# A two-layer graph network on one core: the stretch ahead of the first gather rebuilt, and layer 0's drain reordered

## The chip, the cores and the metric

The kernel runs on one core of a Trainium2 chip. The time is the device time of one execution in microseconds, as the median of several executions; a profile is one execution recorded by the hardware profiler. The core's engines run their own instruction streams and meet at semaphores: PE (matrix product), DVE (vector), ACT (scalar functions), POOL (which here mostly issues gathers) and SP (which issues most DMAs).

## The reference, cut to what matters

The graph has 6250 nodes with 128 features and 106250 edges, sorted by destination. Both layers are computed as `x = x + layer(relu(layernorm(x)))`.

```python
# layer 0: attention over the incoming edges (GATv2)
xl = h @ Wl + bl;  xr = h @ Wr + br
m  = leaky_relu(xl[src] + xr[dst] + edge_weight1 @ We, 0.2)
logits = m @ att
ex    = exp(logits - segment_max(logits, dst)[dst])
alpha = ex / (segment_sum(ex, dst)[dst] + 1e-16)
out = gelu(h + segment_sum(xl[src] * alpha[:, None], dst) + bias_out)   # then a batch norm over all nodes
# layer 1: messages
em = relu(layer_norm(concat(h[src], h[dst]) @ msg_w + msg_b)) * edge_weight
messages = segment_mean(em, dst)
h_new = relu(layer_norm(concat(h, messages) @ upd_w + upd_b));  out = gate * h_new + (1 - gate) * h
```

## The kernel before

**First stretch (L212 to L454).** The nodes are taken in 17 batches of up to three tiles of 128 rows. For batch i a loop over i = 0..18 issues `normal(i)` (ACT makes the normalized rows, L327, and PE transposes them, L328), `product(i - 1)` (ACT copies the transposes, L332, and PE multiplies, L335) and `table(i - 2)` (ACT or DVE copies the product to `tl`, L342, and SP writes it to the DRAM table `xl_d`, L345). Between them stand steps of four generators. `work` (`squeezing`) removes the self loops from the rows of source indices `ed_r`, 99 blocks of 1078 edges: it makes the masks `moves` (L282) and shifts by predicated copies in seven levels (`squeeze`, L210). `stats` makes the layer norm's statistics on DVE (L308, L310). `seen` (`checks`) lets POOL and ACT test whether the graph has the form that the fast code needs, into twelve numbers `bad`; `said` (`verdict`) sums them to a `flag`. `columns_of(q)` transposes the squeezed rows on PE (L415), and DVE turns them into index columns `src_c` (L417, L418). All of it is issued in program order, so the order of the code is the order on each engine.

**Two arms.** Then all engines read the flag, and `tc.If(usual != 0)` (L1798, L1799) runs `fast()`, the Else arm `general()`. The general arm holds some 16,500 instructions and does not run here.

**Set-up of the fast arm (L1030 to L1110).** DVE computes each block's first node (`first_i`, L1045) and relative destinations (`dl_b`, written to `dl_d`), squeezes the edge weights `ea_r` (L210), and makes the tables of `xr` in three bfloat16 parts (`xr_rows`, L1000 to L1006, to `xr_d`); ACT casts the weights to three parts (L1074 to L1083), which SP writes eightfold to `ea_d` (1.58 MB, three DMAs). `load(table, s)` brings a block's node rows (`W`), its destinations (`oht`, 240 KB) and its weight rows (`load_weights`, L1022); `one_hot_t` (L1026) turns the destinations into a transposed one-hot on DVE. SP issues these loads in order with everything else that it sends.

**Layer 0's loop (L1377 to L1457).** 99 blocks s, one round each, and LAG + 1 = 8 rounds more to drain. In a round POOL issues eight gathers of 128 rows of `xl_d` (`gl`, L185); PE expands `xr[dst] + e` (L1124); DVE adds the gathered rows (L1412), ACT applies Relu (L1413), DVE multiplies with `att` (L1422), sums (L1424) and adds (L1425, L1428) to the logits `lgc`. `one_hot_t(s + 2)` stands on DVE between L1412 and L1422 of block s. Four blocks make a batch; `maxima(b)` finds the segment maxima and exponentials of a batch in steps over several rounds (PE `mx` L1165, DVE `lt` L1168, scans, `cc` L1195, `exm` L1208). Seven rounds behind the gathers, block u = s - LAG is aggregated: DVE makes its one-hot `oh` (L1393) and, with ACT, the weighted rows `glw` (L1400 to L1407), PE sums (L1437), ACT copies (L1297) and SP stores to one of two tables `res` (L1127). Groups of four node tiles are finished as their sums are complete (`nodes(g)`, L1216 to L1279): SP fetches `fin`, DVE computes, PE transposes, ACT applies Gelu.

Gathers are paced: with `PACED = 3`, the even gathers of block s wait for successive marks of block s - 3.

```python
marks = passed.get(s - PACED, ())
if j % 2 == 0 and j // 2 < len(marks):          # marks: L1412, L1422, L1428, L1393 of block s - 3
    tc.add_manual_dep(row.ins, marks[j // 2].ins.name, ...)
```

`breaks()` and `late_columns()` are generators whose steps are taken one per round from round 0 on: they prepare the segment boundaries (`fst_d`, `brk_d`, `kbrk`, `brks`), small vectors (`cols`) and the columns of the self loops' weights. Each step sends DMAs on SP's queue, and the first five rounds also send four DMAs of zeros (`res`, 327 KB each).

**The drain.** In the eight last rounds nothing is gathered; the last maxima, the last seven aggregates and the last three node groups (four, three and two tiles) are left. After the loop `in_turn` interleaves the last two groups. A short middle part (batch norm, tables for layer 1) follows, and then layer 1's loop, which is built like layer 0's, with its own gathers from `a_d`.

Of the kernel before, what the change touches and what calls it, by code (L numbers as in the profile page):

```python
# [66 lines left out]
def kernel(  # L67
# [45 lines left out]
    moves = state.tile([NS, 7, BE], U8, name="moves")  # L113
# [3 lines left out]
    own_r = state.tile([NS, RE], F32, name="own_r")  # L117
# [94 lines left out]
    with tc.tile_pool(name="pre", bufs=3) as pp, tc.tile_pool(name="pre1", bufs=1) as p1, tc.tile_pool(  # L212
# [135 lines left out]
        def checks():  # L348
# [5 lines left out]
            acc = p1.tile([NS, 3], F32, name="acc")  # L354
# [3 lines left out]

            place = p1.tile([NS, BE], F32, name="place")
            behind = p1.tile([NS, BE], F32, name="behind")  # L360
            GP.iota(place, pattern=[[1, BE]], base=0, channel_multiplier=0, allow_small_or_imprecise_dtypes=True)
            GP.tensor_scalar(behind, dst_r[:, :BE], base_f, None, op0=ALU.subtract)
            GP.tensor_tensor(place, place, behind, ALU.subtract)
            GP.tensor_scalar(place, place, float(CH), None, op0=ALU.is_le)
            GP.tensor_tensor(place, place, step[:, :BE], ALU.mult)
# [26 lines left out]
            S.activation(junk[:, :BE], place, AF.Copy, accum_out=acc[:, 2:3])  # L392
            GP.tensor_tensor(q, far[:, 0:1], acc[:, 2:3], ALU.subtract)
            GP.tensor_scalar(bad[:, 11:12], q, float(NW - 1), None, op0=ALU.is_gt)
# [6 lines left out]

        def verdict():
            flag_ps = ps_k.tile([1, 12], F32, name="flag_ps", tag="ctp")
            T.matmul(flag_ps, ones[:NS, 0:1], bad, start=True, stop=True)
            yield
            V.tensor_reduce(sum_, flag_ps, AX.X, ALU.add)
            V.tensor_scalar(sum_, sum_, 0.0, None, op0=ALU.is_equal)
            yield
            S.copy(flag, sum_)
# [23 lines left out]
        for i in range(n + 2):  # L433
            if i % 2 and (i + 1) // 2 in rstds:
                scales((i + 1) // 2)
            if i < n:
                normal(i)
            next(stats, None)
            next(work, None)
            if i % 3 == 2:  # L440
                next(work, None)
            if 1 <= i <= n:
                product(i - 1)
            if i == 14:
                for _ in work:
                    pass
            if i in (15, 16):
                columns_of(i - 15)
            if i in (1, 4, 9):
                next(seen)  # L450
            if i >= 11:
                next(said, None)
            if i >= 2:
                table(i - 2)  # L454
# [469 lines left out]
    def fast():  # L924
# [10 lines left out]
        ea_d = dram.tile([NS * 8 * SE], BF16, name="ea_d")  # L935
        base_d = dram.tile([NS * 2], I32, name="base_d")
# [45 lines left out]
        gate = fs.tile([P, NT], F32, name="gate")  # L982
        bns = fs.tile([P, NGR, 6], F32, name="bns")
# [36 lines left out]
        def load_weights(s):  # L1020

            nc.sync.dma_start(ohts[s % 3][KW:P, :], flat(ea_d, [[SE, 8], [1, SE]], s * 8 * SE))  # L1022
# [6 lines left out]
        wins = {}  # L1029
        with tc.tile_pool(name="col1", bufs=1) as p1, tc.tile_pool(name="ps_p", bufs=2, space=PSUM) as ps_p, tc.tile_pool(  # L1030
            name="ps_x", bufs=1, space=PSUM
        ) as ps_x, tc.manual_schedule():
# [19 lines left out]
            squeeze(ea_r, 0)  # L1052
            made = xr_rows(p1, ps, 0)
            next(made)
            for k in range(1, 3):
                squeeze(ea_r, k)
                V.tensor_tensor(we_l, We_r if k == 1 else we_l, we_p[:, k - 1, :], ALU.subtract)
                S.copy(we_p[:, k, :], we_l)
                next(made, None)
# [9 lines left out]
            for k in range(3, 7):  # L1069
                squeeze(ea_r, k)  # L1070
# [13 lines left out]
            for k, (r0, n) in enumerate(((0, 3), (3, 3), (6, 2))):  # L1084
                nc.sync.dma_start(flat(ea_d, [[8 * SE, NS], [SE, n], [1, SE]], r0 * SE),
                                  ea_p[k][:, None, :].to_broadcast([NS, n, SE]))
            for s in range(2):
                load_weights(s)
                one_hot_t(wins[s][1])
            columns(ps_p, eac_c, ea_r, "ctp")  # L1090
# [60 lines left out]
        with tc.tile_pool(name="e0", bufs=2) as ep, tc.tile_pool(  # L1151
# [3 lines left out]
        ) as ps_m, tc.tile_pool(name="ps_1", bufs=1, space=PSUM) as ps_1, tc.manual_schedule():  # L1155
            (iota_ps,) = constants(ps_1)
            LAG = SB + 3
            gls, lgc, exm, pss, aggs, passed = {}, {}, {}, {}, {}, {}

# [56 lines left out]
            def nodes(g):  # L1216
# [44 lines left out]
                for j in range(n):  # L1261
# [38 lines left out]
            def breaks():  # L1300
# [8 lines left out]
                V.tensor_scalar(cut, fst, -BIG, None, op0=ALU.mult)  # L1309
                nc.sync.dma_start(flat(fst_d, [[SE, NS], [1, SE]]), cut)  # L1310
                yield
# [7 lines left out]
                nc.sync.dma_start(flat(brk_d, [[ST, NS], [NS * ST, 3], [1, ST]]), brk)  # L1319
                V.memset(kbrk[:, :, 0:1], 0.0)  # L1320
                V.memset(kbrk[:, :, P : P + 1], 0.0)
                for b, m, n in ((0, NBT, NS // SB), (NS // SB, NS % SB * ST, 1)):
                    if m:
                        nc.sync.dma_start(kbrk[:m, b : b + n, 1:P],
                                          flat(fst_d, [[P, m], [P * NBT, n], [1, P - 1]], b * P * NBT + 1))
                for q in range(2):
# [3 lines left out]
                    S.copy(fst_c[:, :, q * 4 : (q + 1) * 4].rearrange("p s j -> p j s"), tp)  # L1330
                yield
# [8 lines left out]
            def late_columns():  # L1340

                def column(o, a):
# [9 lines left out]
                    yield  # L1352
                V.tensor_add(bias_c, bias_c, bl_c)
                V.tensor_add(wlr, w0[:, :D], w0[:, D:])
                yield from column(own_c[0], own_r)
# [8 lines left out]
                V.tensor_add(wab, w1[:, :D], w1[:, D : 2 * D])  # L1364
                yield
# [11 lines left out]
            for s in range(NS + LAG + 1):  # L1377
# [11 lines left out]
                if 0 <= u < NS:  # L1389
                    b, q = divmod(u, SB)  # L1390
                    m = tiles(u)
                    oh = ep.tile([P, ST, P], F32, name="oh")
                    made_oh = V.tensor_tensor(oh[:, :m, :], over_tiles(iota_ps, m),  # L1393
                                              over_features(dl_c[:, u, :m], m), ALU.is_equal)
                    if s <= NS:
                        passed[s - 1].append(made_oh)
                    if q == 0:
                        next(steps, None)
# [15 lines left out]
                if u < 0 or u % SB:  # L1414
                    next(steps, None)
# [15 lines left out]
                if s + 2 in early:  # L1431
                    made = xr_rows(np_, xp, early[s + 2])
                    next(made)
                if 0 <= u < NS:
# [3 lines left out]
                if s % SB == SB - 1 and s // SB < BT:  # L1438
                    steps = maxima(s // SB)
                next(steps, None)  # L1440
# [10 lines left out]
                if s < 3:  # L1451
                    next(begun)
                else:
# [9 lines left out]
        cen = fs.tile([P, P], F32, name="cen")  # L1463
        V.tensor_scalar(cen, ident, -1.0 / D, None, op0=ALU.add)
        avg = fs.tile([P, 1], F32, name="avg")
        V.memset(avg, 1.0 / D)
        wm = fs.tile([P, D + 1], F32, name="wm")
        V.tensor_copy(wm[:, :D], w1[:, :D])
        V.tensor_copy(wm[:, D:], w1[:, 3 * D : NW1])
# [13 lines left out]
        fx.enter_context(tc.manual_schedule())  # L1483
# [314 lines left out]
    usual = nc.values_load(flag[0:1, 0:1], min_val=0, max_val=1)  # L1798
    with tc.If(usual != 0) as arm:  # L1799
        fast()  # L1800
    with arm.Else():
        general()
# [41 lines left out]
```

## Time and profile before

| what | us |
|---|---|
| median of 3 runs (2247.89 to 2249.55) | 2247.99 |
| the profiled execution | 2248.83 |
| its span | 2247.0 |
| DVE / POOL / ACT / PE busy | 1697.3 / 1575.9 / 1283.9 / 1160.8 |
| first gather of layer 0 | 69.31 |
| last gather of layer 0 ends | 1084.83 |
| last logits (L1428 of block 98) | 1091.41 |
| batch norm's aggregate (L1491) | 1145.69 |
| first gather of layer 1 | 1193.53 |
| last output issued | 2240.88 |

The span runs from the first to the last instruction of the record; the execution's own time lies 1.83 us above it. Times on a timeline are from the span's start. A timeline row gives start, duration, engine, line and operation, `out<-in` by tile names, and in brackets how long the engine stood idle before the row and what released it. A row with x2 or more is several equal instructions in sequence. A row of waits reads: who waited for whom, total us, number of waits, the longest.

### The profile page before, as it was taken

The numbers are of one execution on the slowest core, as the hardware profiler recorded it, in microseconds if no ns is written. First come the engines' busy times: TensorE is split into PE (matmuls) and PEld (weight loads), VectorE is DVE, ScalarE is ACT, GpSimd is POOL, SyncE is SP. The second block draws the span as 40 slices with busy tenths as digits, with TensorE's granted clock in tenths as the row PEclk, the third lists the DMA queues.
The fourth block names the chain that finished last, engine by engine and source line by source line (L and its number), as shares of the span: only waits on it lengthen the run. The fifth ranks groups of instructions, "written<-read, shape, count | busy, mean of one in ns | idle before, by whom it ended". The sixth has DMA issues, their size and how long they took to land. (4 is left out here: it accounts for less than half of the span.)

```text
span 2247.0 us, 28217 instructions
## 1 busy us (share of the span) xinstructions
PE 1160.8 (52%) x6261; PEld 1032.2 (46%) x6261; DVE 1697.3 (76%) x3898; ACT 1283.9 (57%) x4314; POOL 1575.9 (70%) x1637
## 2 busy tenths in 40 slices
PE   5215545645555654655673445454554554554454
PEld 4114545544444544544553445454544554544443
DVE  8558887887787787777864677787787787788785
ACT  6214434444443444433435677777787787787774
POOL 6667777777777777777226777777777777777770
PEclk9556666665666566555676666666666665766776
DMA  5463356434444434434223333443443343343341
GB/s 139 143 187 100 94 150 187 123 93 113 114 94 115 111 88 114 118 84 107 49 61 104 87 104 94 106 113 93 107 109 101 96 115 106 87 117 104 95 106 30
DMA packets 243495, 239.16 MB, mean 106 GB/s; under 512 B 90708, under 2 KB 186909, under 8 KB 243315
## 3 DMA queue, kind: packets, MB, share of 16 engines
q1 hardware_dynamic: 192531, 133.21, 21.0%
q0 software_dynamic: 50496, 103.92, 19.7%
q14 instruction: 128, 1.05, 0.2%
q8 instruction: 52, 0.85, 0.2%
q10 hardware_dynamic: 288, 0.13, 0.0%
HBM read 189.20 MB, written 47.90 MB: 106 GB/s over the span
## 5 line engine op out<-in xcount | busy, mean ns | idle before, releaser
L185 POOL DMA_INDIRECT gl<-xl_d,src_c x789 | 767.2, 972 | 267.3 <-issue 162.2
L185 POOL DMA_INDIRECT gl<-a_d,src_c x789 | 752.7, 954 | 248.7 <-issue 166.4
L1437 PE MATMUL agg_ps<-glw,oh 128*128 128x131 f32 x1578 | 342.8, 403 | 217.0 <-ACT agg L1297 154.1
L1437 PEld LDWEIGHTS agg_ps<-glw,oh 128*128 128x128 f32 x1578 | 318.7, 306 | 238.3 <-ACT agg L1297 219.4
L1774 PE MATMUL agg_ps<-glw,oh 128*128 128x130 f32 x1056 | 240.9, 417 | 331.5 <-ACT glw L1765 331.5
L1774 PEld LDWEIGHTS agg_ps<-glw,oh 128*128 128x128 f32 x1056 | 222.5, 314 | 345.5 <-ACT glw L1765 345.5
L1745 ACT ACTIVATE sq<-y 128x128 f32<-128x128 f32 x789 | 243.8, 309 | 107.9 <-DVE y L1737 86.1
L1407 ACT ACTIVATE glw<-gl,exm 128x128 f32<-128x128 f32 x763 | 233.1, 389 | 0.0
L1413 ACT ACTIVATE m_ps<-m_ps 128x1024 f32<-128x1024 f32 (+1 forms) x99 | 99.5, 1005 | 218.0 <-DVE m_ps L1412 109.9
L1412 DVE TENSOR_TENSOR m_ps<-m_ps,gl 128x1024 f32<-128x1024 f32 (+1 forms) x99 | 121.7, 1230 | 123.6 <-DMA gl<-xl_d,src_c 107.3
L1756 DVE SCALAR_TENSOR_TENSOR y<-y,rs,cst 128x128 f32<-128x128 f32 x789 | 211.7, 341 | 0.0
L1774 PE MATMUL agg_ps<-ea_r,oh 128*128 128x130 f32 x522 | 120.4, 421 | 171.3 <-ACT ea_r L1765 171.3
L1124 PEld LDWEIGHTS <-oht 128*128 128x128 bf16 (+1 forms) x1578 | 146.2, 126 | 124.7 <-issue 55.5
L1774 PEld LDWEIGHTS agg_ps<-ea_r,oh 128*128 128x128 f32 x522 | 111.0, 318 | 177.9 <-ACT ea_r L1765 177.9
L1026 DVE TENSOR_SCALAR oht<-oht,third 120x1024 bf16<-120x1024 bf16 x198 | 100.1, 506 | 103.7 <-DMA oht<-dl_d 103.5
L1765 ACT ACTIVATE glw<-y,ew_c 128x128 f32<-128x128 f32 x528 | 161.5, 388 | 0.0
L1422 DVE TENSOR_TENSOR m_ps<-m_ps,att 128x1024 f32<-128x1024 f32 (+1 forms) x99 | 120.9, 1221 | 36.9 <-ACT m_ps L1413 36.2
L1745 ACT ACTIVATION_READ_ACCUMULATOR sq<-y 128x1 f32 x789 | 146.9, 186 | 0.0
L1737 DVE TENSOR_TENSOR y<-y_ps,gl 128x1024 f32<-128x1024 f32 (+1 forms) x99 | 119.4, 1206 | 33.2 <-DMA gl<-a_d,src_c 17.3
L1124 PE MATMUL m_ps<-W,oht 128*128 128x128 bf16 x789 | 89.2, 282 | 101.4 <-DVE lr L1424 83.0
L1761 ACT ACTIVATE y<-y 128x1024 f32<-128x1024 f32 (+1 forms) x99 | 104.3, 1054 | 37.6 <-DVE y L1758 37.6
L1424 DVE TENSOR_REDUCE lr<-m_ps 128x8 f32<-128x1024 f32 (+1 forms) x99 | 120.9, 1221 | 3.4
(329 smaller groups left out, 2247.2 us busy)
## 6 DMA issues: line engine op xcount, KB each, us to landing
oht<-dl_d SPq DMA_DIRECT2D x198, 240.0 KB
gl<-xl_d,src_c POOLq DMA_INDIRECT x789
gl<-a_d,src_c POOLq DMA_INDIRECT x789
res<-zt SPq DMA_DIRECT2D x20, 327.5 KB
res<-zt SPq DMA_DIRECT2D x20, 325.0 KB
res<-agg SPq DMA_DIRECT2D x99, 64.5 KB
res<-agg SPq DMA_DIRECT2D x99, 64.0 KB
W<-xr_d SPq DMA_DIRECT2D x198, 30.0 KB
```

What stands on the lines that cost most here:

```text
L185: return GP.indirect_dma_start(out=dest, out_offset=None, in_=table, in_offset=bass.IndirectOffsetOnAxis(ap=idx, axis=0))
L1124: T.matmul(ps[:, j, :], oht[:rows_, j * P : (j + 1) * P], w[:rows_, j // TN, :], start=True, stop=True)
L1407: S.activation(glw[:, j, :D], glu[:, j, :D], AF.Copy, scale=f)
L1412: passed[s] = [V.tensor_tensor(ps, ps, gl[:, :n, :D], ALU.add)]
L1422: passed[s].append(V.tensor_tensor(ps, ps, over_tiles(att8, n), ALU.mult))
L1424: V.tensor_reduce(lr, ps, AX.X, ALU.add)
L1437: T.matmul(aggs[u], oh[:, j, :], glw[:, j, :], start=(j == 0), stop=(j == m - 1))
L1737: added = V.tensor_tensor(y[:, :n, :], pss.pop(s)[:, :n, :], gl[:, :n, :], ALU.add)
L1745: S.activation(sq, y[:, j, :], AF.Square, accum_out=rs[:, j : j + 1])
L1756: marks.append(V.scalar_tensor_tensor(yu[:, j, :], yu[:, j, :], ru[:, j : j + 1], mg_ps, op0=ALU.mult, op1=ALU.mult))
L1765: S.activation(glw[:, j, :D], yu[:, j, :], AF.Copy, scale=ew_c[:, u, j : j + 1])
L1774: T.matmul(aggs[u], oh[:, j, :], glw[:, j, :], start=(j == 0), stop=(j == m - 1))
```

## The change

It has six parts.

1. `checks` loses the tests that used `place` and `behind` (seven POOL instructions and ACT's sum L392); three small DVE instructions on one column of the squeezed rows take their place in `bad[11]`. The flag now counts violations, `general()` is the If arm and `fast()` the Else arm.
2. In the first stretch the squeezing ends at i = 12 (14 before), `columns_of` stands at 13 and 14 (15 and 16), and the first three of the seven squeezes of `ea_r` move from the fast arm's set-up to i = 16, 17 and 18, ahead of `table(i - 2)`.
3. The weights of the first four blocks go to a table `ea_h` of their own, sent ahead of the whole of `ea_d`, and `load_weights` reads it for s < 4. The whole `ea_d` follows the first two loads.
4. The order written by hand holds from the fast arm's start. `cen`, `avg` and `wm` are made in the last steps of `late_columns`.
5. `breaks` has four steps instead of three, with its DMAs a step later; `late_columns` begins in round 3 beside the fourth.
6. Drain: the last maxima start in round NS, two steps at a time and ahead of the aggregate in PE's order. The one-hots of the last three blocks are made in rounds 85, 87 and 89 into buffers that are free by then. For the last three node groups, two of the three products per node tile go to ACT.

```diff
-            place = p1.tile([NS, BE], F32, name="place")
-            behind = p1.tile([NS, BE], F32, name="behind")
-            GP.iota(place, pattern=[[1, BE]], ...)
-            GP.tensor_scalar(behind, dst_r[:, :BE], base_f, None, op0=ALU.subtract)
-            GP.tensor_tensor(place, place, behind, ALU.subtract)
-            GP.tensor_scalar(place, place, float(CH), None, op0=ALU.is_le)
-            GP.tensor_tensor(place, place, step[:, :BE], ALU.mult)
...
-            S.activation(junk[:, :BE], place, AF.Copy, accum_out=acc[:, 2:3])
-            GP.tensor_tensor(q, far[:, 0:1], acc[:, 2:3], ALU.subtract)
-            GP.tensor_scalar(bad[:, 11:12], q, float(NW - 1), None, op0=ALU.is_gt)
...
+            V.tensor_scalar(half_i, ed_r[:, CH : CH + 1], P - 1, None, op0=ALU.bitwise_and)
+            V.tensor_tensor(more, far[:, 0:1], half_i, ALU.subtract)
+            V.tensor_scalar(bad[:, 11:12], more, float(NW - 1), None, op0=ALU.is_gt)
...
-            if i == 14:
+            if i == 12:
                 for _ in work:
                     pass
-            if i in (15, 16):
-                columns_of(i - 15)
-            if i in (1, 4, 9):
+            if i in (1, 4, 9, 12):
                 next(seen)
-            if i >= 11:
+            if i in (13, 14):
+                columns_of(i - 13)
+            if i >= 16:
+                squeeze(ea_r, i - 16)
+            if i >= 13:
                 next(said, None)
             if i >= 2:
                 table(i - 2)
...
-            nc.sync.dma_start(ohts[s % 3][KW:P, :], flat(ea_d, [[SE, 8], [1, SE]], s * 8 * SE))
+            nc.sync.dma_start(ohts[s % 3][KW:P, :],
+                              flat(ea_h if s < SB else ea_d, [[SE, 8], [1, SE]], s * 8 * SE))
...
-            squeeze(ea_r, 0)
+            squeeze(ea_r, 3)
             made = xr_rows(p1, ps, 0)
             next(made)
             for k in range(1, 3):
-                squeeze(ea_r, k)
...
-            for k in range(3, 7):
+            for k in range(4, 7):
                 squeeze(ea_r, k)
...
+            send(ea_h, 0, SB)
             for s in range(2):
                 load_weights(s)
                 one_hot_t(wins[s][1])
+            send(ea_d, 0, NS)
...
+                if g >= NGR - 3:
+                    for j in range(n):
+                        for o, k in ((fin[:, 1, j, :D], 1), (xl[:, j, :D], 2)):
+                            S.activation(o, o, AF.Copy, scale=mm[:, k, j : j + 1])
+                    for j in range(n):
+                        V.scalar_tensor_tensor(fin[:, 0, j, :D], fin[:, 0, j, :D], mm[:, 0, j : j + 1],
+                                               fin[:, 1, j, :D], op0=ALU.mult, op1=ALU.add)
+                    V.tensor_tensor(fin[:, 0, :n, :D], fin[:, 0, :n, :D], xl[:, :n, :D], ALU.add)
-                for j in range(n):
+                for j in range(n if g < NGR - 3 else 0):
                     V.tensor_scalar(fin[:, 0, j, :D], fin[:, 0, j, :D], mm[:, 0, j : j + 1], None, op0=ALU.mult)
...
                 V.tensor_scalar(cut, fst, -BIG, None, op0=ALU.mult)
+                yield
                 nc.sync.dma_start(flat(fst_d, [[SE, NS], [1, SE]]), cut)
-                yield
...
+                    if q == 0 and s >= NS:
+                        next(steps, None)
+                        if s == NS:
+                            steps = maxima(BT - 1)
+                            next(steps)
+                    elif s > NS:
+                        next(steps, None)
+                        next(steps, None)
+                    oh = ohs.pop(u, None)
+                    if oh is None:
+                        oh = ep.tile([P, ST, P], F32, name="oh")
+                        made_oh = one_hot(oh, u)
...
+                if 85 <= s < 91 and s % 2:
+                    k = (s - 85) // 2
+                    ohs[NS - 3 + k] = rooms[k]
+                    one_hot(rooms[k], NS - 3 + k)
+                if s >= NS:
+                    next(steps, None)
+                    next(steps, None)
                 if 0 <= u < NS:
                     aggs[u] = ps_1.tile([P, WF], F32, name="agg_ps")
...
-    usual = nc.values_load(flag[0:1, 0:1], min_val=0, max_val=1)
-    with tc.If(usual != 0) as arm:
+    special = nc.values_load(flag[0:1, 0:1], min_val=0, max_val=12 * P)
+    with tc.If(special != 0) as arm:
+        general()
+    with arm.Else():
         fast()
-    with arm.Else():
-        general()
```

## The prediction

> **What bounds the kernel now.** I read the page first, then POOL's waits and timeline, then what stands ahead of the first gather, then the drain. Times below are the profiled execution's: span 2247.0, execution 2248.83, which is 0.84 above the median 2247.99.
>
> The page's costliest groups (busy us, mean ns | idle before):
>
> ```profile
> L185 POOL DMA_INDIRECT gl<-xl_d,src_c x789 | 767.2, 972 | 267.3 <-issue 162.2
> L185 POOL DMA_INDIRECT gl<-a_d,src_c x789 | 752.7, 954 | 248.7 <-issue 166.4
> ```
>
> A gather costs 0.94 to 0.95 us and 0.30 of issue, 1.25 in all; 789 of them make 986 us of the 1015.5 us in which layer 0 gathers (69.31 to 1084.83). So layer 0 is POOL's: a microsecond counts if it moves the first gather, opens or closes a gap between gathers, or lies behind the last. DVE, at 76%, mostly does not count. POOL's waits in layer 0 and the rows behind the two long ones:
>
> ```profile
> POOL gl L185 <- DVE first_i L1045: 19.0, 1, 19.0
> POOL gl L185 <- DVE m_ps L1422: 12.1, 13, 8.5
> ...
> 69.31 1.45 POOL L185 DMA_INDIRECT gl<-xl_d,src_c  x1 [18.95 <-DVE first_i L1045]
> ...
> 147.06 0.94 POOL L185 DMA_INDIRECT gl<-xl_d,src_c  x1 [8.46 <-DVE m_ps L1422]
> ```
>
> Bracketed is the idle time before a row and its releaser. The first wait is put down to first_i, but a gather reads xl_d and src_c; DVE's row of the same moment names the landing. From DVE's timeline:
>
> ```profile
> 59.08 0.86 DVE L417 CAST ed_c<-ctp 128x396 int32<-128x396 f32 x1 [6.51 <-PE ctp L415]
> ...
> 64.93 0.29 DVE L342 COPY tl<-mm 128x129 f32<-128x129 f32 x1 [0.48 <-PE mm L335]
> 65.80 0.69 DVE L1039 TENSOR_SCALAR ed_r<-ed_r 99x1024 int32<-99x1024 int32 x1 [0.58 <-issue]
> ...
> 68.41 0.23 DVE L1464 TENSOR_SCALAR cen<-ident 128x128 f32<-128x128 f32 x1 [1.90 <-DMA xl_d<-tl]
> ...
> 145.16 0.48 DVE L1026 TENSOR_SCALAR oht<-oht,third 120x1024 bf16<-120x1024 bf16 x1 [14.07 <-DMA oht<-dl_d]
> 145.57 1.23 DVE L1422 TENSOR_TENSOR m_ps<-m_ps,att 128x1024 f32<-128x1024 f32 x1
> ```
>
> Last table copy 64.93, table landed 68.41, first gather 69.31: 4.4 us from copy to gather. And gather 50 (block 6, third tile; each block's even gathers are paced by block s-3) waits for block 3's L1422, which stands behind a one-hot whose load came late. The drain, again from DVE's timeline:
>
> ```profile
> 1100.67 0.28 DVE L1168 COPY lt<-mx 21x128 f32<-21x128 f32 x1 [4.52 <-PE mx L1165]
> ...
> 1129.25 0.17 DVE L1237 TENSOR_TENSOR own_l<-fin 128x3 f32<-128x3 f32 x1 [4.04 <-DMA fin<-res]
> ```
>
> DVE idles 4.52 because mx is queued on PE behind a node group's eight `up` pairs and an aggregate, and 4.04 because the next group is fetched only when block 96 is stored.
>
> **1. The first stretch.** Seven POOL steps over 99x1078 go, five of them from 18.46 to 32.60 without a break, and ACT's L392 (1.10+0.19). While they run, DVE is slow: L282 takes 1.73, 1.45 and 1.95 (later 0.69 to 0.72), L210 2.83 (next 1.34), L318 0.91 (0.17). Up to 29.3, where ACT waits for DVE for the last time (3.73), that is 1.0+0.75+1.5+0.74 = 4.0 us. From there ACT works without a gap until 58.5, so its end moves by 4.0+1.3 = 5.3, to about 53.2. The columns (L417, L418) come two batches earlier, 1.95 us each, so at about 59.08-5.3-3.9 = 49.9 instead of at the end, where they held table copies back (PE waited 1.80 and 1.92 for them). Their place on DVE is taken by three squeezes of 1.35, 1.37 and 1.42, each ahead of a table copy. DVE from 53.4: copy 0.55, squeeze, copy, squeeze, copy, squeeze, last copy at about 59.3. Plus 4.4: first gather 63.7, **-5.6**. Bounds: -3 if POOL's 2.23 us product (L396), now at about 33, slows DVE there in its turn; -8 if the squeezes fit into DVE's waits. POOL's moved checks end at 50.4 already, so POOL itself waits for nothing new; the three tiny DVE steps are 0.5 us inside the 6.51 that DVE waits.
>
> **2. The branch.** The general arm is now the near one; all engines jump over it. The nearest row is the test without a jump: 0.58 us idle ahead of L1039. For POOL a jump lies inside its wait of 18.95 for the table; for DVE and SP it delays the setup by 0 to 3 us, which section 3 covers. At the end a jump falls away: the last output is issued at 2240.88+0.29, a landing takes about 3.1 (65.27 to 68.41), and the span ends at 2247.0, so at most some 2.7 us can be in it. I take the value nearest the row, **-0.5** (0 to -2.7).
>
> The Trainium skill, "Runtime: NRT & Kernel Launch", section "Instruction fetch mechanics", speaks against this edit: a taken branch out of the two fetched pages stalls until the target page is fetched. By that rule every engine pays at the start what it saved at the end; POOL's share stays hidden, so the total would be the same or lower by that stall. No row here shows a fetch by itself.
>
> **3. The early rounds.** After the branch three squeezes (4.14) are gone from the setup and it starts 5.6 earlier, so the node table xr_d leaves at about 67 (76.32 before). The weights go through a small table of four blocks: its three sends follow the casts (87.15 before, about 77 now), and the first loads need not wait until 1.58 MB have landed (issued 83.2 to 87.5, read at 93.77). First L1412 at about 83 (97.16). The price is queue order: the full 1.58 MB now stand on SP ahead of load(2), so one_hot(2), and L1422(0) behind it on DVE, wait until about 89 (99.46 before). From there the rounds were set by loads: DVE waited 5.62, 7.41 and 14.07 for them, because SP had been held by fst_d (waiting for DVE's cut), brk_d, xr_d, zeros and five small columns. With fst_d and brk_d each sent a round later, load(3) goes past them; I get L1422(1) at 98 (113.1), L1422(2) at 104 (126.5) and, with xr_d, four zeros, brk_d and kbrk now ahead of load(5), L1422(3) at 120 (145.57). Gather 50 is due at 137.66+0.94+0.30-5.6 = 133.3. That leaves 13 us, so the gap of 8.46-0.30 = **-8.1** closes. Bounds: 0 to -8.1. What is late next: gather 58 needs L1422(4), about 131 against 143. The slow first ten gathers (about 7 us above 1.25 each) I leave as they are.
>
> Added to later rounds: three one-hots of 1.22 us in rounds 85, 87 and 89. A round is 10 us of POOL with DVE busy 77%, so 2.3 us are free: 0. The copies for cen, avg and wm, some 0.6 us, likewise.
>
> **4. The drain.** All relative to the same start (L1428 of block 98 at 1091.41). lt no longer waits for the aggregate of 3.48: 1097.4 instead of 1100.67. But one one-hot and its products (2.1 us) that filled DVE before lt now stand behind it, the middle of the maxima waits for the aggregate that is now behind mx (cc about 1101.8, about 1.5 us of idle in two places), and two blocks' one-hot and products lie ahead of the four-tile group's end instead of one. Its products: twelve DVE steps (3.95 from 1113.07) become eight ACT copies of 0.30 with a sum at the end, 2.45+0.7 = 3.15. PE's four transposes, which ran between products, now all wait for the sum: 1.6. I get the aggregate of block 96 at 1118.7 to 1119.4 (1120.02), its end 1121 to 1122.5 (1123.9), and own_l of the three-tile group, 5.4 us behind it by store and fetch, at 1127.3: -1.9. That group then saves 0.4 (2.92 becomes 1.85+0.6). In the two-tile group ACT's products stand behind a table load of 1.28 and a gelu of 0.52 (1140.52 to 1142.33) and PE's transposes behind the sum: +0.7. Drain **-1.6**; bounds +2 (PE slow, ACT in the way) and -7.8 (4.5 of idle and three one-hots, 1.22+1.22+0.82, gone whole).
>
> **Sum.** -5.6-0.5-8.1-1.6 = -15.8; 2248.83-15.8 = 2233.0, and 0.84 less on the scale of the median: **2232**. All behind the drain only moves.
>
> **Rivals.** (a) The gap returns: load(2) behind 1.58 MB, or a jump of 3 us on SP, and L1422(3) arrives after 141.5. Against it are 13 us of slack; for it, that every wait of these rounds was a load. Then -5.6-0.5-1.6 = -7.7: 2240. (b) The drain pays what its edits remove, -7.8 instead of -1.6: 2226. For it, all of DVE's 4.52 is PE's order; against it, the fetch behind block 96. (c) Slower: gathers stretch while DVE copies; beside L210 at 148.7 to 151.5 two took 1.29 and 1.12 instead of 0.94. If the new DVE order (late columns' squeezes, one-hots) stretches layer 0's mean from 972 to above 972+15.8/789 = 992 ns, the gain is gone; at 1000 ns it is 22 us, so 2254. Against it: the long steps are as many as before. (d) The change doesn't do what it says: the table copies stay bound by PE and the first gather stays at 69, with the gap closed: 2238.
>
> **How the numbers follow.** The forecast 0.70, (a) 0.12, (b) 0.08, (c) 0.05, (d) 0.05. The forecast's own bounds in sections 1, 2 and 4 give 2225 to 2239; (b) with the earliest first gather reaches 2223, (a) with its own spread 2243. Differences under 0.2%, 4.5 us, are no change here: faster 0.90, same 0.05, slower 0.05.
>
> **What would show it.** First gather near 63.7; no wait above 1 us on L185 but the first; L1422(3) near 120; gathers ending near 1071; from the last L1428 to bn_aggr 52 to 53 us (54.3 before); L185's mean at 972 or under. I am wrong if the first gather is after 66, if a gap above 3 us stands anywhere in layer 0, or if the drain is longer than before.

## The result and the profile after

| what | before | after | difference |
|---|---|---|---|
| median (4 runs each) | 2247.94 | 2226.64 | ratio 0.9902, 95% interval 0.9885 to 0.9919 |
| lowest and highest | 2246.44, 2249.55 | 2223.24, 2226.99 | |
| the profiled execution; its span | 2248.83; 2247.0 | 2226.99; 2225.2 | span -21.8 |
| first gather | 69.31 | 64.26 | -5.05 |
| layer 0's gathers, first start to last end | 1015.52 | 1006.67 | -8.85 |
| last gather's end to the last logits | 6.58 | 6.66 | +0.08 |
| drain, last logits to the batch norm's aggregate | 54.28 | 52.56 | -1.72 |
| middle, from there to layer 1's first gather | 47.84 | 45.47 | -2.37 |
| layer 1, to the last output's issue | 1047.35 | 1045.39 | -1.96 |
| tail, to the span's end | 6.12 | 4.19 | -1.93 |

The seven stages add up to the span's 21.8. The experiments below ran on three chips. On the second and the third every kernel took about a quarter longer, before included (2795 and 2840), so whole times are compared only within a chip. The extra time lies in the two loops: layer 0's gathers take 1236 to 1260 us there and 1003 to 1010 in the changed kernel and its variants on chips of normal speed, layer 1 takes 1349 to 1385 against 1045 to 1048. The first stretch, the drain and the middle take about what they take elsewhere and are compared across chips.

Of the profile after, first the page's costliest groups, then POOL's waits (who waited for whom, total us, times, longest):

```profile
L187 POOL DMA_INDIRECT gl<-xl_d,src_c x789 | 766.5, 971 | 267.5 <-issue 169.5
L187 POOL DMA_INDIRECT gl<-a_d,src_c x789 | 753.9, 956 | 248.0 <-issue 178.9
```

```profile
POOL gl L187 <- DVE first_i L1050: 27.3, 1, 27.3
```

A gather costs what it cost (971 ns against 972, 956 against 954), and the wait that stood second, 12.1 us for the product with att, has gone. The first wait is longer (18.95 before) only because POOL, without its tests, is idle from 36.93 on instead of 50.36. Two stretches of DVE's timeline, the end of the first stretch and the early rounds:

```profile
51.31 0.88 DVE L414 CAST ed_c<-ctp 128x396 int32<-128x396 f32 x1 [3.70 <-PE ctp L412]
...
58.63 1.42 DVE L212 COPY_PREDICATED ea_r<-moves,ea_r 99x1074 f32<-99x1074 uint8 x1
59.89 0.33 DVE L344 COPY tl<-mm 128x129 f32<-128x129 f32 x1
62.90 0.69 DVE L1044 TENSOR_SCALAR ed_r<-ed_r 99x1024 int32<-99x1024 int32 x1 [2.69 <-issue]
...
94.26 0.57 DVE L1030 TENSOR_SCALAR oht<-oht,third 120x1024 bf16<-120x1024 bf16 x1 [8.77 <-DMA oht<-dl_d]
94.75 1.21 DVE L1461 TENSOR_TENSOR m_ps<-m_ps,att 128x1024 f32<-128x1024 f32 x1
...
128.09 0.49 DVE L1030 TENSOR_SCALAR oht<-oht,third 120x1024 bf16<-120x1024 bf16 x1 [12.15 <-DMA oht<-dl_d]
128.50 1.22 DVE L1461 TENSOR_TENSOR m_ps<-m_ps,att 128x1024 f32<-128x1024 f32 x1
```

The last table copy came 5.04 us earlier (59.89 against 64.93), and the gather followed 4.37 behind it (4.38 before). New is the 2.69 us in which DVE waits for nothing that the profile shows, just where it now jumps over the general arm. The one-hots of the early rounds still wait for their loads, but no gather does. POOL's timeline at the first gathers and at gather 50:

```profile
64.26 1.21 POOL L187 DMA_INDIRECT gl<-xl_d,src_c  x1 [27.33 <-DVE first_i L1050]
...
130.94 0.94 POOL L187 DMA_INDIRECT gl<-xl_d,src_c  x1 [0.30 <-issue]
...
142.70 1.87 POOL L187 DMA_INDIRECT gl<-xl_d,src_c  x1 [0.30 <-issue]
```

Gather 50, which had waited 8.46, starts 0.30 behind its neighbour. Its condition, the product at 128.50, was fulfilled at about 129.7, 1.2 us ahead of it: the gap closed by a hair. The drain, on DVE:

```profile
1083.60 0.28 DVE L1184 COPY lt<-mx 21x128 f32<-21x128 f32 x1 [3.67 <-PE mx L1181]
...
1113.49 0.16 DVE L1253 TENSOR_TENSOR own_l<-fin 128x3 f32<-128x3 f32 x1 [5.05 <-DMA fin<-res]
...
1130.15 0.51 DVE L1530 BATCH_NORM_AGGREGATE bmv<-bns 128x2 f32<-128x78 f32 x1
```

The first idle time shrank from 4.52 to 3.67, the second, for the fetch behind the last but two blocks, grew from 4.04 to 5.05: part of what was taken away came back there.

### The profile page after: what moved, and what is told of

The parts are those of the page before. It is cut to its first block, busy times and chain, and to the rows that moved or that the text cites. A ratio compares the mean times of both kernels' runs of the same rounds, so it can differ in the third digit from the quotient of the medians.

```text
span 2225.2 us, 28204 instructions
## 1 busy us (share of the span) xinstructions
PE 1142.5 (51%) x6261; PEld 1018.4 (46%) x6261; DVE 1688.0 (76%) x3885; ACT 1288.1 (58%) x4330; POOL 1564.2 (70%) x1630
## 5 line engine op out<-in xcount | busy, mean ns | idle before, releaser
L1483 PE MATMUL agg_ps<-glw,oh 128*128 128x131 f32 x1536 | 328.7, 398 | 216.6 <-ACT agg L1321 177.6
L1483 PEld LDWEIGHTS agg_ps<-glw,oh 128*128 128x128 f32 x1536 | 306.4, 302 | 236.8 <-ACT agg L1321 219.4
L1813 PEld LDWEIGHTS agg_ps<-glw,oh 128*128 128x128 f32 x1056 | 221.6, 313 | 349.3 <-ACT glw L1804 349.3
L1452 ACT ACTIVATE m_ps<-m_ps 128x1024 f32<-128x1024 f32 (+1 forms) x99 | 99.5, 1005 | 214.9 <-DVE cc L1211 111.0
L1461 DVE TENSOR_TENSOR m_ps<-m_ps,att 128x1024 f32<-128x1024 f32 (+1 forms) x99 | 120.9, 1221 | 38.8 <-ACT m_ps L1452 38.0
```

What stands on the lines that cost most here:

```text
L1461: passed[s].append(V.tensor_tensor(ps, ps, over_tiles(att8, n), ALU.mult))
L1483: T.matmul(aggs[u], oh[:, j, :], glw[:, j, :], start=(j == 0), stop=(j == m - 1))
L1813: T.matmul(aggs[u], oh[:, j, :], glw[:, j, :], start=(j == 0), stop=(j == m - 1))
```

## The experiments

Each is the changed kernel with one edit or one group of edits, and all compute everything. Times of stages are each from one profiled execution.

**The fast arm near again.**

```diff
+            V.tensor_scalar(sum_, sum_, 0.0, None, op0=ALU.is_equal)
-    special = nc.values_load(flag[0:1, 0:1], min_val=0, max_val=12 * P)
-    with tc.If(special != 0) as arm:
-        general()
-    with arm.Else():
-        fast()
+    usual = nc.values_load(flag[0:1, 0:1], min_val=0, max_val=1)
+    with tc.If(usual != 0) as arm:
+        fast()
+    with arm.Else():
+        general()
```

> The changed kernel with the fast arm as the near one again, as before the change; nothing else. Changed kernel: DVE idle 2.69 us ahead of its first instruction in the arm, first gather 64.26, last output issued 2221.01, span end 2225.2 (4.2 us later; 6.1 in the kernel before). Theory (the jump costs at the start but is hidden for POOL, and its absence saves about 1.9 us at the end): idle ahead of DVE's first step back to about 0.6, first gather within 0.3 of 64.26, last output to end about 6.1, execution 1 to 2 us longer. Rival (the 1.9 us at the end are something else): last output to end stays near 4.2, execution within 1 us.

2230.22 (one run; before on that chip 2250.34). DVE no longer idles behind the last table copy:

```profile
60.45 0.28 DVE L344 COPY tl<-mm 128x129 f32<-128x129 f32 x1
60.64 0.68 DVE L1045 TENSOR_SCALAR ed_r<-ed_r 99x1024 int32<-99x1024 int32 x1
```

and from the last output's issue to the end it takes 6.86 instead of 4.19. So the idle time at 60.2 and the 2.7 us at the end are both the price of a jump, and the one that the change pays is covered: the first gather is at 64.15 against 64.26, the first block's addition (L1452) at 82.84 against 84.26.

**POOL's tests back.** The seven steps with `place` and `behind` and ACT's sum are restored, the three small DVE steps removed; all else as changed.

```diff
+            GP.iota(place, pattern=[[1, BE]], ...)
+            GP.tensor_scalar(behind, dst_r[:, :BE], base_f, None, op0=ALU.subtract)
...
+            S.activation(junk[:, :BE], place, AF.Copy, accum_out=acc[:, 2:3])
```

> The changed kernel with POOL's and ACT's old test (place, behind, L392's sum) back; all else as changed. Theory (DVE runs slow beside POOL's 99x1078 steps, ACT is released late): DVE's masks in the first 33 us take 1.5 to 1.9 us instead of 0.69, first gather 4 to 5 us later than 64.26; the stretch of gathers moves as a whole, gap ahead of gather 50 under 2 us. Rival (the gain of the first stretch is the moved index columns alone): first gather at most 1 us later.

2228.83. The last table copy is at 63.86 and the first gather at 68.36, 4.1 us later than in the changed kernel; no gap appears (gather 50 at 136.15). DVE's first three masks take 1.73, 1.45 and 1.95 again, as before the change (0.69 to 0.73 without the tests). Of the 5.05 at the first gather these tests are therefore some 4; ACT's sum is among them and was not tried alone. About 1 is left for the moved columns and squeezes together.

This run also settles a rival for the closed gap, that only the earlier start of the set-up closes it. Here the set-up starts at 66.84, later than before the change (65.80). The products with att of blocks 0 and 3, in the kernel before and then in this run:

```profile
99.46 1.23 DVE L1422 TENSOR_TENSOR m_ps<-m_ps,att 128x1024 f32<-128x1024 f32 x1 [0.69 <-ACT m_ps L1413]
145.57 1.23 DVE L1422 TENSOR_TENSOR m_ps<-m_ps,att 128x1024 f32<-128x1024 f32 x1
```

```profile
98.73 1.21 DVE L1467 TENSOR_TENSOR m_ps<-m_ps,att 128x1024 f32<-128x1024 f32 x1
132.99 1.23 DVE L1467 TENSOR_TENSOR m_ps<-m_ps,att 128x1024 f32<-128x1024 f32 x1
```

The first comes at nearly the same time, the fourth 12.6 us earlier. What closed the gap lies between the first block and the fourth.

**The three squeezes back in the set-up.**

```diff
-            if i >= 16:
-                squeeze(ea_r, i - 16)
...
-            squeeze(ea_r, 3)
+            squeeze(ea_r, 0)
             made = xr_rows(p1, ps, 0)
             next(made)
             for k in range(1, 3):
+                squeeze(ea_r, k)
```

> The changed kernel with the first three squeezes of the edge weights back in the fast arm's set-up (4.2 us of DVE work ahead of the last table copies gone). Theory (these squeezes, not PE or ACT, set the last table copy): last copy at about 56 instead of 59.89, first gather 3 to 4 us earlier (about 60.7); the set-up is longer by what it starts earlier, so block 3's second step stays near 128.5 and gather 50, due at about 127, waits 2 to 3 us: execution within 2 us of the changed kernel. Rival (PE sets the last copy): first gather within 0.5 of 64.26, block 3's step near 132, gap about 3 us, execution 3 us longer.

2232.68, and neither expectation held. The last table copy came 2.6 us earlier (57.3), yet the first gather did not (64.48). What changed was the next gather, beside two of the returned squeezes. POOL's and then DVE's timeline of this run:

```profile
64.48 2.01 POOL L187 DMA_INDIRECT gl<-xl_d,src_c  x1 [27.51 <-DVE dl_b L1052]
66.80 4.19 POOL L187 DMA_INDIRECT gl<-xl_d,src_c  x1 [0.30 <-issue]
```

```profile
62.32 0.69 DVE L1042 TENSOR_SCALAR ed_r<-ed_r 99x1024 int32<-99x1024 int32 x1 [4.73 <-issue]
...
65.94 1.38 DVE L212 COPY_PREDICATED ea_r<-moves,ea_r 99x1076 f32<-99x1076 uint8 x1
...
68.01 1.38 DVE L212 COPY_PREDICATED ea_r<-moves,ea_r 99x1074 f32<-99x1074 uint8 x1
```

A gather of 0.94 took 4.19, as one did before the change:

```profile
72.32 4.15 POOL L185 DMA_INDIRECT gl<-xl_d,src_c  x1 [0.30 <-issue]
```

From first to eleventh gather it is 20.13 us here, 19.53 before, 15.65 in the changed kernel. The moved squeezes pay by not standing beside the first gathers: 4.5 us. The Trainium skill, "SBUF — State Buffer", section "SBUF: two separate sides", says that POOL cannot write the descriptors of its DMAs while DVE runs an operation in a mode that takes both ports. Its example is an fp32 copy. No run here shows the ports; these rows show a gather stretched beside predicated copies. Not every such copy does it: in the changed kernel two gathers beside the three predicated copies from 71.05 to 73.72 took 0.96 and 0.94.

**One weight table.** The small table's three sends are gone; the whole `ea_d` is sent ahead of the first two loads.

```diff
-            send(ea_h, 0, SB)
+            send(ea_d, 0, NS)
...
-            send(ea_d, 0, NS)
...
-                              flat(ea_h if s < SB else ea_d, [[SE, 8], [1, SE]], s * 8 * SE))
+                              flat(ea_d, [[SE, 8], [1, SE]], s * 8 * SE))
```

> The changed kernel without the small table: the whole 1.58 MB of weights go ahead of the first loads, which read them. Theory (the small table buys an early first block but not the rounds behind it, since the second load stands behind the same 1.58 MB in both): block 0's first step at about 90 instead of 84.26, its second step within 3 us of 94.75, block 3's second step within 4 us of 128.5, gap ahead of gather 50 under 4 us. Rival (the small table is what closed the gap): block 3's second step at 137 or later, gap over 6 us, execution 6 us longer or more.

2224.04. The first block's addition came 5.1 us later (89.40 against 84.26), but the products with att came at 94.06, 102.89, 110.65 and 127.88 against 94.75, 103.54, 111.30 and 128.50, and there is no gap. The 1.58 MB must pass either ahead of the first loads or behind them; in this run the small table was worth nothing.

**Squeezes into DVE's idle time,** far arm and near arm. The three steps stand at i = 13 instead of 16 to 18, where DVE waits for the columns; once as changed otherwise, once with the near arm.

```diff
+            if i == 13:
+                squeeze(ea_r, 0)
+                squeeze(ea_r, 1)
             if i in (13, 14):
                 columns_of(i - 13)
+            if i == 13:
+                squeeze(ea_r, 2)
-            if i >= 16:
-                squeeze(ea_r, i - 16)
```

> The changed kernel with the first three squeezes of the edge weights moved once more: two into the 3.70 us in which DVE waits for the first transposes of the index rows, one behind those columns, so none stands ahead of a table copy; arms as changed. With the squeezes back in the set-up the last table copy came at 56.83, but the first gather stayed at 64.48. Theory A (the taken branch holds POOL as well, to about 64): last copy at 57 to 58, first gather still 64.0 to 64.6, the first ten gathers 15.7 as in the changed kernel; execution within 2 us of the changed kernel's. Theory B (POOL waits for the landing, and what held it with the squeezes back was the set-up): first gather 61 to 62, execution 2 to 3 us shorter.

> The same three squeezes in DVE's wait, and the fast arm as the near one. Theory A (the branch holds POOL): first gather at the landing, about 61 to 62, since no jump is left; DVE's set-up starts at about 58; gather 50 still finds block 3's step done or waits under 1.5 us; the end of the span is again 6 to 7 us behind the last output. Theory B (the branch is hidden for POOL): first gather as in squeezes_idle, within 0.4.

> The same kernel as near_idle (fast arm near, the three moved squeezes put into DVE's wait ahead of the columns' copies), on another chip. Last table copy near 57.3, DVE's first step of the arm near 58.6 with no idle time ahead of it. Theory A (with the copies earlier, the landing of the table and the engines' jump are what is late, each by itself enough to hold the first gather at 64): with both gone, the first gather comes at 61 to 62. Rival (the landing is bound by the writes themselves, some 0.8 MB left when the last four batches go out together from 55.7 on): first gather at 63.5 or later although everything on DVE is earlier. Tail 6.5 to 7 us against 4.2, as in arms_near. Time: about that of the changed kernel, within 3 us.

Far arm: 2780.32; last table copy at 58.2, 5.50 us of idle time at the jump, first gather 64.75. Near arm: 2775.29 on the same chip, and 2829.7 (median of 10) on the third, 7 us above the changed kernel there, where within 3 was expected. The two ranges overlap (2812.22 to 2838.19 against 2814.47 to 2828.60); 2.4 of the 7 is the jump at the end, 6.52 from the last output's issue against 4.15. The last copies are at 58.0 and 58.5, the arm begins at 58.77 and 59.63, and yet the first gather is at 67.50 and 65.50, later than in the changed kernel's own run on the third chip (63.99). With both the late copy and the jump gone, the gather was no earlier, and the 61 to 62 of the theories did not come. SP's timeline of the second near run:

```profile
56.69 2.87 SPq L347 DMA_DIRECT2D xl_d<-tl  x4
60.81 0.35 SPq L1055 DMA_DIRECT2D base_d<-first_i  x1
61.53 0.30 SPq L1059 DMA_DIRECT2D dl_d<-dl_b  x1
65.32 0.21 SPq L1060 DMA_DIRECT2D base_row<-base_d  x1
```

The four last table writes are sent by 59.56, and the gather starts 5.9 us behind that, where the changed kernel has 3.7 (60.57 to 64.26). By these rows the landing is late, not the sending. (`base_row`, which reads `base_d`, leaves 4.5 us behind it, which is no longer than the 4.6 before the change and the 5.2 in the changed kernel, and shows nothing.) That agrees with the rival stated for this run, that the writes themselves bound it. What exactly holds them was not measured, and no run of a near arm with early copies was had on a chip of normal speed, so the cause stays open.

**The drain of before** in the changed kernel: last maxima behind the aggregate in PE's order and from the usual round, one-hots in their own rounds, all products on DVE.

> The changed kernel with layer 0's drain as before: last maxima in the old place, the three one-hots in their own rounds, all products on DVE. From the last logits to the batch norm's aggregate the changed kernel took 52.56, the kernel before 54.28; three variants whose drain is the changed one took 49.44 to 52.49. Theory (the drain's edits are worth 1 to 3 us, the rest is PE's clock): 54 to 55 here. Rival (the edits are worth what they remove from DVE, 8 us): 58 or more, or, the other way, 52 or less if they are worth nothing.

> The same kernel as drain_old (the changed kernel with the drain of before: last maxima after the loop's rounds, one-hots in their own rounds, products on DVE), on another chip and in several rounds beside the changed kernel itself. Theory (the drain's edits are worth about 2 us): from the last logits to bn_aggr 52.5 to 54.5 us, where the changed kernel has 50 to 52.6; the median 1 to 4 us longer than that of the changed kernel. Rival (they are worth the idle time that they remove, 7.8): 57 us or more, and the median 6 us longer. Rival (worth nothing: the changed kernel's own spread covers it): drain and median the same within 1 us.

2793.01 once; median 2821.77 of 10 against 2822.57 for the changed kernel beside it: the whole time cannot tell them apart on that chip, where single runs of the changed kernel spread from 2814.47 to 2828.60, and the 1 to 4 us that the median was expected to lose did not show. By stages they differ:

| kernels | drain | middle | both |
|---|---|---|---|
| before; drain of before (two runs) | 54.28; 52.49, 51.99 | 47.84; 48.94, 48.92 | 102.12; 101.43, 100.91 |
| changed drain, 11 kernels' profiles | 49.31 to 52.56 | 45.14 to 48.20 | 94.45 to 98.03, median 97.27 |

The sums of the two groups do not overlap, though the drains alone do. By stages the drain's edits are worth some 4 us, 101.43 less 97.27, half of it behind the drain. No run of the changed kernel with the old drain was had on a chip of normal speed.

What spreads the drains of one kind is PE's granted clock at their start. Eight pairs of products `up` stand there ahead of the last `mx`. One step of them in the changed kernel, and in the run with one weight table:

```profile
1078.21 0.80 PE L1247 MATMUL up<-wlr,h_sb 128*128 128x128 f32 x2
```

```profile
1074.09 0.49 PE L1246 MATMUL up<-wlr,h_sb 128*128 128x128 f32 x2
```

Over the `up` products and `mx` the mean granted clock is 0.50 in the changed kernel and with the near arm, 0.53 in the kernel before, and 0.60 to 0.99 in all others. From the last logits to `lt` it takes 9.26 before the change and 6.01 and 6.10 with the new drain at the low clock; above it, 7.43 and 6.98 with the old drain and 3.33 to 3.94 with the new. Like compared with like, the drain itself gained 1.7 us at the low clock (54.28 to 52.56) and some 2 above it (52.49 and 51.99 against a median of 50.08).

The reason for the half behind the drain is in PE's timeline just behind the batch norm's aggregate, which is the same code. Before:

```profile
1149.31 3.78 PE L1514 MATMUL ctr<-x_sb,cen 128*128 128x512 f32 x4 [0.91 <-DVE x_sb L1509]
1152.88 1.71 PE L1545 MATMUL var_ps<-avg,sq 128*128 128x1 f32 x8
1154.45 2.07 PE L1550 MATMUL mm<-wm,h_sb 128*128 128x129 f32 x8
```

After:

```profile
1133.77 3.78 PE L1553 MATMUL ctr<-x_sb,cen 128*128 128x512 f32 x4 [0.91 <-DVE x_sb L1548]
1137.34 1.10 PE L1584 MATMUL var_ps<-avg,sq 128*128 128x1 f32 x8
1138.30 1.14 PE L1589 MATMUL mm<-wm,h_sb 128*128 128x129 f32 x8
```

The granted clock, 0.50 in both while PE mostly waits, is full 3.9 us behind the first `ctr` row in the changed kernel (at 1137.65) and 8.9 us behind it in the kernel before (at 1158.19). In the three profiles with the old drain the eight products with avg took 1.70 to 1.71, in ten of the eleven with the new one 0.95 to 1.36 (the eleventh, with the squeezes back in the set-up, has 1.71). The stretch at 0.50 that ends there lasts 20.5 us in those ten and 23.9 us in the other four, so this half comes as one step of the clock and not in proportion to the edits. Why the clock comes up at another moment was not tested.

**The DMAs of `breaks` in their old places.**

```diff
                 V.tensor_scalar(cut, fst, -BIG, None, op0=ALU.mult)
-                yield
                 nc.sync.dma_start(flat(fst_d, [[SE, NS], [1, SE]]), cut)
+                yield
...
-                yield
-                nc.sync.dma_start(flat(brk_d, ...), brk)
...
-                if s < 4:
+                if s < 3:
                     next(begun)
-                if s >= 3:
+                else:
                     next(late, None)
```

> The changed kernel with breaks in three steps, its DMAs where they were (fst_d in round 0, brk_d and kbrk in round 1, brks and columns in round 2, late columns from round 3). Theory (SP's queue set the early rounds: a load behind a DMA that waits for DVE comes late): block 1's and block 2's second steps later by 3 us or more than 103.54 and 111.3, block 3's at 135 or later against 128.5, gap ahead of gather 50 of 4 us or more, execution 4 us longer. Rival (the earlier start alone closed the gap, the order on SP changes little): block 3's second step within 2 us of 128.5, no gap above 1 us.

> The same kernel as breaks_old (the DMAs of the segment boundaries sent in the steps where before had them), on another chip. Theory (SP's order sets the early rounds): the second and third blocks' product with att come 5 us or more later than in the changed kernel (103.5, 111.3), the fourth after 134 (128.5 in the changed kernel), and gather 50 waits 3 to 9 us, which lengthens the run by as much. Rival (the early first gather and the small table alone close the gap): no wait over 1 us ahead of any gather but the first, and the median as the changed kernel's.

2782.80 once; median 2823.88 of 10 against 2822.57 for the changed kernel. The products with att of the first four blocks, on the third chip: 94.81, 112.83, 125.54 and 144.72, against 94.92, 105.78, 128.16 and 144.49. So the old order costs the second block 7 us, and by the fourth nothing is left of it. On the second chip the old order had the first four at 93.95, 111.60, 128.92 and 148.46, the kernel with the drain of before (new order) at 94.26, 103.06, 124.18 and 140.47: there 8 us remained, though block 3 of the two kernels with the squeezes in DVE's idle time came at 143.50 and 147.72. The theory held for where the rounds move, not for the time: gather 50 waited 9.48 and 9.85 with the old order, but 6.61 to 7.67 in the other kernels of these two chips. The long waits of the gathers up to the 50th, the first apart, add up to 16.6 us with the old order against 15.9 on the third chip, and 20.0 against 12.4 to 16.0 on the second.

On chips of normal speed the old order was not run, but the other runs there leave little else. From block 0's product with att to block 3's it takes 46.1 us before the change and 33.7 to 34.3 in the five kernels with the new order, and gather 50 waits in none of these five. The tests back, the squeezes back and the one table change neither. Of the change's parts only the order of the DMAs of `breaks` is left in these rounds.

**The changed kernel once more,** as the measure on the third chip.

> The changed kernel itself once more, as the measure for the other three runs on this chip: first gather 64 to 65, no gap in layer 0, drain 49.5 to 52.6, tail 4.2, median 2223 to 2228. If the shares by stage come out as in its first profile, the unforecast 2.4 us of the middle part and 2.0 of layer 1 belong to the kernel; if they spread by as much, they are the spread of single executions.

Median 2822.57 (before 2839.77; ratio 0.9941, 0.9917 to 0.9965). First gather 63.99, drain 50.38, middle 47.04. The gaps that were not expected are there: gathers 42 and 50 waited 9.25 and 6.65 for products behind late loads. The middle is 1.6 longer than in the first profile and still 1.9 shorter than with the drain of before on this chip (48.92).

## Why the prediction was right, and where its terms were off

The forecast was 2232 with 2223 to 2243; 2226.64 is faster and inside. The forecast's sum was -15.8 against a span shorter by 21.8.

**First stretch, -5.6: measured -5.05.** The chain held: POOL's tests gone, the three slow masks at 0.69 to 0.73 (L284), columns at 51.31 (49.9 forecast), last copy at 59.89 (59.3), gather 4.37 behind. The bound named for the product of POOL is there too: one squeeze beside it took 3.49. What the working had wrong is the fixed 4.4 us from copy to gather. With the squeezes back in the set-up it was 7.2, so a still earlier copy brought nothing there, and the end of the range at -8 was out of reach by that way.

**Branch, -0.5: measured -1.93 in the tail.** A jump has a price after all, 2.7 us, at both ends; I took the value nearest a row that held no jump. The Trainium skill's rule ("Runtime: NRT & Kernel Launch", "Instruction fetch mechanics") agrees with DVE's 2.69 and with the arms' exchange; the fetch itself no row shows. What it leaves to the trace is the cover: at the start the jump lies beside the wait for the table, so nothing of it was paid.

**Early rounds, -8.1: measured -8.15, with the slack wrong.** Gather 50 waits no more, but L1461 of block 3 came at 128.50, not 120, and the 13 us of slack were 1.2. The failed step is SP's queue, which was named and not timed. Most of the 8.5 us stood at block 0 already: its product came at 94.75, not 89, behind a one-hot that waited 8.77 us for load(2), and load(2) left behind the 1.58 MB. Block 1 was 5.5 us late, block 2 7.3. SP's timeline after:

```profile
104.26 0.30 SPq L1025 DMA_DIRECT2D oht<-ea_d  x1
115.47 0.42 SPq L1009 DMA_DIRECT2D xr_d<-tab_p  x1
115.94 1.99 SPq L1103 DMA_DIRECT2D res<-zt  x4
117.97 1.10 SPq L1351 DMA_DIRECT2D brk_d<-brk  x1
119.18 2.76 SPq L1354 DMA_DIRECT2D kbrk<-fst_d  x2
...
124.00 0.41 SPq L1020 DMA_DIRECT2D oht<-dl_d  x1
```

SP stood 11 us for `tab_p`, whose source DVE made only behind block 2's late product (L1007 at 114.11), and load(5) behind it left at 124.00. Rival (a) was thus nearer than its 0.12: on the slower chips a gap of 6 to 10 us stood there in every kernel.

**Not in the sum: the first ten gathers, -3.9.** "I leave as they are" was the step that failed most. The moved squeezes were costed on DVE alone; that they left the stretch where POOL gathers was not seen, although the 4.15 us gather stood in the trace beside them. Against it stand +3.2 us of longer gathers in the rest of layer 0, such as the 1.87 at 142.70 beside two predicated copies of 2.77 us: rival (c)'s mechanism, a seventh of its size. In the four other kernels on chips of normal speed the same gathers are only -0.3 to +1.7 off the kernel before, so most of the 3.2 is what single executions spread. -3.9, -8.15 and +3.2 make the -8.85 of the table.

**Drain, -1.6: measured -1.72.** From the last logits, `lt` was forecast at 6.0 and came at 6.01, the three-tile group's own_l at 35.9 and came at 35.90. Rival (b), -7.8, gave the number 2226 and not the reason. The match to a hundredth is luck: the working took its rows at the low clock, the profile after had the same clock, and in the nine profiles above it `lt` comes at 3.33 to 3.94. The clock at the drain's start, which the working does not name, moves this term by more than the term: all 11 profiles with the new drain lie between 49.31 and 52.56.

**"All behind the drain only moves": -2.37 and -1.96 instead of 0.** The first is the clock described above. Layer 1 took 1045.4 to 1048.2 in the five kernels of the normal chips whose layer 1 is the same code, so its -1.96 lies within what it spreads by itself.

So it is partly luck that the total lies inside the range: -3.9, -2.4 and -2.0 came unforecast, and +3.2 against them. The range's lower end was also not added up rightly: the bounds of sections 1, 2 and 4 together give 2221, not 2225.

No version run here beats the changed kernel by more than its own spread, as far as they can be compared: one weight table gave 2224.04 in a single run, inside 2223.24 to 2226.99. On the second chip the changed kernel itself was not run.

## What to carry to other kernels

Cost a moved step on every engine that it stops standing beside, not only on the one that runs it: the three squeezes cost DVE the same in both places and POOL some 4 us in one. When a gap is closed by changing a queue's order, time the queue itself, row by row, up to the transfer that opened the gap, or a slack of 13 us turns out to be 1. Put the far jump where a long transfer is being waited for anyway. And before a stage is compared between two profiles, look at the granted clock at its start.

## What the runs showed of the hardware

- An idle time of 2.4 to 2.8 us, for which the profile shows no reason, on DVE at the jump over the general arm (2.69 in the changed kernel), and of 3.7 to 4.2 on ACT. When DVE came to the jump earlier it was 4.73 and 5.50, and ended at 62.3 and 64.0; with POOL's tests back it was 2.69 and ended at 66.84. What sets its length was not tried.
- A gather of 0.94 us stretches to 4.19 beside predicated copies of 99x1076 and 99x1074, but not beside every predicated copy (0.96 and 0.94 beside those at 71.05).
- The same PE code, at a clock of 0.50 when it starts, gets the full clock 3.2 to 4.4 us later in ten profiles and 8.9 to 9.6 in four, and the stage behind it differs by about 2 us.
- The same two products `up` take 0.80 us at a granted clock of 0.50 and 0.49 at 0.99.
